# Maxima of cross-attention scores turned in two groups of 64 partitions, and modulation rows with the conditions stationary

## The chip, the core and the metric

The kernel runs on one core of a Trainium2 chip. A core has five engines, each with a queue of its own that is worked in order: TensorE (PE, with its weight loads PEld shown apart), VectorE (DVE), ScalarE (ACT), GpSimd (POOL) and SyncE (SP), which here issues DMAs. TensorE multiplies a stationary operand, loaded beforehand, by a moving one that streams past it, and writes to PSUM. A transpose ("turn" in the kernel) is such a product: the data stationary, a unit matrix moving.

The metric is device time in microseconds of the whole program.

## What is computed

One transformer block with adaptive layer norm: 16 batches of 224 tokens of width 512, 16 heads of 32, a context of 750 tokens. All in float32. Cut to what matters:

```python
c_proj = silu(c) @ W_mod + b_mod
shift_a, scale_a, gate_a, shift_m, scale_m, gate_m = split(c_proj, 6)
x_norm = ln(x) * (1 + scale_a[:, None]) + shift_a[:, None]
q, k, v = heads(x_norm @ W_qkv + b_qkv)
x = x + gate_a[:, None] * (heads_joined(softmax(q @ k.T * scale) @ v) @ W_proj + b_proj)
q_c = heads(ln(x) @ W_qc + b_qc)
k_c, v_c = heads(ln(context) @ W_kvc + b_kvc)
x = x + (heads_joined(softmax(q_c @ k_c.T * scale) @ v_c) @ W_cproj + b_cproj)
h = gelu((ln(x) * (1 + scale_m[:, None]) + shift_m[:, None]) @ W_mlp1 + b_mlp1)
x = x + gate_m[:, None] * (h @ W_mlp2 + b_mlp2)
```

The change touches two places: `c_proj`, and the maximum that the softmax of the cross attention takes over the 750 context tokens and subtracts before exp.

## The kernel before

It runs in four stages one after the other: a head (loads, modulation, first norms), self attention, cross attention, and the MLP. `Ordered` (line 22) keeps every engine's instructions in the order of the program; all of them are recorded on its line 28, so the profile is read by the names of the tiles. The `plan` dictionaries are a schedule written by hand: `at_slot` puts projections, norms and loads of the next step between the pieces of the present one.

**Modulation.** W_mod is loaded in six parts of 512 columns (`load_part`), two buffers for them. `make_part` (line 279) makes one part. Parts 2 and 5 are gates: the turned conditions `c_t` (128 x 16 per piece) are stationary and 512 columns of W_mod move; the rows get their bias and go to DRAM. Parts 0, 1, 3, 4 (shift and scale of attention and MLP) have W_mod stationary, in 16 blocks of 128 x 128, and the 16 columns of `c_t` moving, so that the result is at once by column (`mod_t`), 16 conditions wide. Parts 0 and 1 are made in the head (line 597), before x is turned and modulated (`turn_x`); 3 and 4 in slots of the first pair of batches. All biases come as rows into `brow` by five DMAs on ScalarE's queue at the start (line 138), and are turned to columns `bcol` by one transpose (line 270). `c_in`, the conditions, is loaded after them on the same queue; Silu of it, `c_act`, is then turned to `c_t`.

**Cross attention.** 64 units, 16 batches times 4 groups of 4 heads (`Unit`, line 964). A unit makes scores in three steps of two context chunks of 125 tokens: `scores(n)` with context tokens on the partitions, `keep(n)` folds them into the running maximum `top` (VectorE; 125 partitions, 4 heads x 224) and copies them to `pt` (ScalarE). At the unit's end `maxima` (line 1004) turns `top` by eight transposes of 125 partitions, in two PSUM banks one after the other, and reduces each bank on VectorE to `mc`, the negated maximum per head and token, with tokens on the partitions. `split_max` on GpSimd then writes it as three bfloat16 terms into three columns of `nmc`, whose other columns are zero.

In the next unit, the one before is worked on: `max_row` (line 1022) turns `nmc` by eight bfloat16 transposes, ScalarE copies the result to `mrow`, and `subtract(h)` (line 1031), once for each half of the heads, spreads it over 125 partitions by a bfloat16 product with ones (448 columns) and adds it to the three `pt` on VectorE. `weights(h)` takes exp on ScalarE and sums on GpSimd. One unit later still, `values` and `finish` make the output. So three units are in flight, and the order on every engine is the one of the loop at line 1085. PSUM: `sc` one buffer of four banks, `mm` three of one bank, `o` one.

Of the kernel before, what the change touches and what calls it, by code (L numbers as in the profile page):

```python
# [8 lines left out]
F32 = mybir.dt.float32  # L9
BF16 = mybir.dt.bfloat16  # L10
# [27 lines left out]
def kernel(  # L38
# [35 lines left out]
    CP = 125  # L74
    CC = S // CP
    CH = CC // 2
    PB = 2
    NP = B // PB
    PT = PB * TC
# [29 lines left out]
    nc.gpsimd.memset(ones16, 1.0)  # L109

    nms = []
    for i in range(3):
        t = const.tile([TP, TC, HG, HD], BF16, name=f"nm{i}")
        nc.gpsimd.memset(t, 0.0)
        nms.append(t)

    nmc = const.tile([TP, HG, TC, P], BF16, name="nmc")
    nc.gpsimd.memset(nmc, 0.0)  # L120

    def split_max(engine, nm, m):

        r = small.tile(list(m.shape), F32, name="rest")
        engine.tensor_copy(nm[:, :, :, 0], m)
        engine.tensor_tensor(r, m, nm[:, :, :, 0], ALU.subtract)
        engine.tensor_copy(nm[:, :, :, 1], r)
        engine.tensor_tensor(nm[:, :, :, 2], r, nm[:, :, :, 1], ALU.subtract)

# [3 lines left out]
    o_mlp = o_kvc + 2 * KC  # L135
    nbias = o_mlp + NF
    brow = const.tile([nbias, P], F32, name="brow")
    for off, vec in ((o_mod, b_mod), (o_qkv, b_qkv), (o_qc, b_qc), (o_kvc, b_kvc), (o_mlp, b_mlp1)):
        rows = vec.shape[0] // P
        nc.scalar.dma_start(out=brow[off : off + rows, :], in_=vec.rearrange("(r p) -> r p", p=P))  # L140
    bcol = const.tile([P, nbias], F32, name="bcol")

    def bias_rows(pool, vec, rows, name):
# [108 lines left out]
        xs[b] = load_x(sa, tokens(x, b), 6)  # L252
    load_part(1)
    wq, wk, wv = (load_w(ws, w_qkv[:, i * H : (i + 1) * H], f"wqkv{i}") for i in range(3))
    bg = mp.tile([B, 2, H], F32, name="bg", bufs=1)
    for i in range(2):
        lo = (2 + 3 * i) * H
        nc.scalar.dma_start(out=bg[:, i, :], in_=b_mod[lo : lo + H].partition_broadcast(B))

    c_act = mp.tile([B, H], F32, name="c_act", bufs=1)  # L260
    nc.scalar.activation(c_act, c_in, AF.Silu)

    c_t = mp.tile([P, KC, B], F32, name="c_t", bufs=1)
    ps = ps_mm.tile([P, 512], F32, name="mm")
# [1 line left out]
        turn(ps[:, k * B : (k + 1) * B], c_act[:, k * P : (k + 1) * P], ident[:B, :B])  # L266
    nc.vector.tensor_copy(c_t.rearrange("p k b -> p (k b)"), ps[:, : KC * B])

    ps = ps_mm.tile([P, 512], F32, name="mm")
    turn(ps[:, :nbias], brow, ident[:nbias, :nbias])  # L270
    nc.vector.tensor_copy(bcol, ps[:, :nbias])
    for i in (1, 4):
        sl = bcol[:, o_mod + i * KC : o_mod + (i + 1) * KC]
        nc.vector.tensor_scalar(sl, sl, 1.0, None, ALU.add)

    bqc = const.tile([P, KC], F32, name="bqc")
    nc.vector.tensor_scalar(bqc, bcol[:, o_qc : o_qc + KC], SCALE, None, ALU.mult)

    def make_part(i):
        w = w_part[i]  # L280
        ps = ps_mm.tile([P, 512], F32, name="mm")
        if i % 3 == 2:
            for k in range(KC):
                mm(ps[:B, :H], c_t[:, k, :], w[:, k, :], start=(k == 0), stop=(k == KC - 1))
            g = mp.tile([B, H], F32, name="gates", bufs=1)
            nc.vector.tensor_tensor(g, ps[:B, :H], bg[:, i // 3, :], ALU.add)
            nc.sync.dma_start(out=gate_d[i // 3], in_=g)
        else:
            slot = (i // 3) * 2 + i % 3
            for m in range(KC):  # L290
                for k in range(KC):
                    mm(
                        ps[:, m * B : (m + 1) * B], w[:, k, m * P : (m + 1) * P], c_t[:, k, :],
                        start=(k == 0), stop=(k == KC - 1),
                    )
            for m in range(KC):
                nc.vector.tensor_scalar(
                    mod_t[:, slot * KC + m, :], ps[:, m * B : (m + 1) * B],
                    bcol[:, o_mod + i * KC + m : o_mod + i * KC + m + 1], None, ALU.add,
                )  # L300
# [133 lines left out]
    if True:  # L434
# [70 lines left out]
        for p in range(NP):  # L505
            if p < NP - 1:
                for g in range(1, KC):
                    at_slot(p, 2 * g - 2, 0, lambda p=p, g=g: whole(project_qk(p, g)))
                    at_slot(p, 2 * g - 2, 1, lambda p=p, g=g: whole(project_qk(p, KC + g)))
                for t in range(PT if p else 0):  # L510
                    at_slot(p, 1 + t // 2 * 2, t % 2, lambda p=p, t=t: whole(project(p - 1, t)))
            else:

                left = [(project_qk, p, m) for m in (1, KC + 1, 2, KC + 2)]
                left += [(project, p - 1, t) for t in range(2)]
                left += [(project_qk, p, m) for m in (3, KC + 3)]
                left += [(project, p - 1, t) for t in range(2, PT)]
                parts = [h for f, *args in left for h in halves(lambda f=f, args=args: f(*args))]
                for i, h in enumerate(parts):
                    at_slot(p, i // 3, i % 3 // 2, h)  # L520
            if p == 0:
                at_slot(p, 1, 0, lambda: make_part(2))
                at_slot(p, 1, 1, lambda: make_part(3))
                at_slot(p, 1, 1, lambda: load_part(4))
                at_slot(p, 1, 1, lambda: load_part(5))
                at_slot(p, 3, 0, lambda: make_part(4))
                at_slot(p, 3, 1, lambda: make_part(5))
                at_slot(p, 3, 1, load_cross)
            n = p + 1
            if n < NP:  # L530
                if n > 1:
                    at_slot(p, 0, 0, lambda n=n: fetch(n))
                at_slot(p, 1, 0, lambda n=n: norm_begin(n))
                for t in range(PT):
                    at_slot(
                        p, 1 + t // 2, t % 2, lambda n=n, t=t: norms[PB * n + t // TC].stats(t % TC)
                    )
                for j in range(PB):
                    at_slot(p, 1 + j, 1, lambda n=n, j=j: norms[PB * n + j].apply())
                for k in range(KC):  # L540
                    at_slot(p, 4, k // 2, lambda n=n, k=k: turn_x(n, k))
                for t in range(PT):
                    at_slot(p, 5 + t // 2, t % 2, lambda n=n, t=t: project_v(n, t))
                at_slot(p, 7, 0, lambda n=n: whole(project_qk(n, 0)))
                at_slot(p, 7, 1, lambda n=n: whole(project_qk(n, KC)))

        def self_scores(p, g, j, nm):
# [12 lines left out]
                sc[:TP, :, : TC * N].rearrange("p s (c t) -> p s c t", c=TC),  # L560
                AX.X, ALU.max, negate=True,
            )
            split_max(nc.vector, nm, m)

        def self_weights(p, g, j, row):
            return weights_t(
# [27 lines left out]
        norm_begin(0)  # L594
        for j in range(PB):
            norms[j].all()
        make_part(0)
        make_part(1)
        load_part(2)
        load_part(3)  # L600
        fetch(1)
# [209 lines left out]
    with tc.tile_pool(name="ca", bufs=2, reuse_waits="tile") as ca:  # L811
# [152 lines left out]
        class Unit:  # L964
# [37 lines left out]
                self.pts.append(pt)  # L1002

            def maxima(self):
                m = small.tile([TP, HG, TC], F32, name="mc")
                for h in range(2):
                    ps = ps_mm.tile([P, 512], F32, name="mm")
                    for s in range(2):
                        for c in range(TC):
                            lo = (s * TC + c) * CP  # L1010
                            turn(
                                ps[:TP, lo : lo + CP], self.top[:, 2 * h + s, c * TP : (c + 1) * TP],
                                ident[:CP, :CP],
                            )
                    nc.vector.tensor_reduce(
                        m[:, 2 * h : 2 * h + 2, :],
                        ps[:TP, : 2 * TC * CP].rearrange("p (s c t) -> p s c t", s=2, c=TC),
                        AX.X, ALU.max, negate=True,
                    )
                split_max(nc.gpsimd, nmc, m)  # L1020

            def max_row(self):
                ps = ps_mm.tile([P, 1024], BF16, name="mm")
                for s in range(HG):
                    for c in range(TC):
                        lo = s * N + c * TP
                        turn(ps[:, lo : lo + TP], nmc[:, s, c, :], ident16[:TP, :TP])
                self.row = ca.tile([P, HG * N], BF16, name="mrow", bufs=1)
                nc.scalar.copy(self.row, ps[:, : HG * N])

            def subtract(self, h):

                bc = ps_o.tile([P, 512], F32, name="o")
                mm(
                    bc[:CP, : 2 * N], ones16[:, :CP], self.row[:, 2 * h * N : 2 * (h + 1) * N],
                    start=True, stop=True,
                )
                less = bc[:CP, : 2 * N].rearrange("p (s t) -> p s t", s=2).unsqueeze(2)
                for pt in self.pts:
                    w4 = pt[:, 2 * h : 2 * h + 2, :].rearrange("p s (k t) -> p s k t", k=2)  # L1040
                    nc.vector.tensor_tensor(w4, w4, less.to_broadcast([CP, 2, 2, N]), ALU.add)
# [43 lines left out]
        for b, g in units:  # L1085
# [2 lines left out]
                last.values()  # L1088
            for n in range(CH):
                st = cur.scores(n)  # L1090
                if n == 0 and prev:
                    prev.max_row()
                if n == 0 and last:
                    last.finish()
                cur.keep(n, st)
# [10 lines left out]
        sc = ps_s.tile([P, HG, 512], F32, name="sc")  # L1106
        prev.values()
        mlp_plain(sc[:, 0], 0)
        cur.max_row()
        prev.finish()  # L1110
        mlp_plain(sc[:, 1], 1)
        cur.subtract(0)
# [200 lines left out]
```

## Time and profile before

| | us |
|---|---|
| runs shown | 2943.93, 2943.95, 2952.13 (median 2943.95) |
| the profiled execution | 2940.97 |
| its span, first to last instruction | 2939.2 |
| mean granted clock of TensorE | 0.991 of full |
| turns of top: `mm<-ident,top`, 512 of 0.271 | 65.8 busy |
| turns of nmc: `mm<-ident,nmc`, 512 of 0.216 | 37.0 busy |
| products with ones: `o<-mrow,ones`, 128 of 0.355 | 45.4 busy |
| copies to mrow in cross attention (ScalarE), 64 of 0.906 | 58.0 busy |
| reductions to mc (VectorE), 128 of 0.669 | 85 busy |
| modulation, W_mod stationary: `mm<-c_t,w_mod`, 128 of 0.318 | 21.3 busy |
| modulation, conditions stationary: `mm<-w_mod,c_t`, 16 of 0.674 | 8.4 busy |

The profile gives groups of instructions as output<-inputs, with stationary rows*columns, and the moving shape. A float32 product is recorded as two instructions, a transpose as one. Durations of TensorE hold its pipeline's tail, so neighbours overlap; what a stream costs is read from start to start. A window's line gives the busy time of each engine in it, then the granted clock, the share of DMA time and GB/s. A wait's line says who waited for whom, how long in all, how often, and the longest.

### The profile page before, as it was taken

Reading aid. Unit: us, or ns where it says so; the run is one execution under the profiler, and the core shown is the slowest. Engines: PE = TensorE matmul, PEld = TensorE weight load, DVE = VectorE, ACT = ScalarE, POOL = GpSimd, SP = SyncE. Lnnn points to the kernel's source line nnn. Section 1 sums busy time; section 2 is a strip of 40 time slices with the busy share of each in tenths; the row PEclk is TensorE's granted clock in tenths of the full one; section 3 lists DMA queues with packets and bytes.
Section 4 is the critical chain, followed back from the end, with each engine's and each line's share of the span. In section 5 each row is a group of like instructions: output and inputs, shape, how many; then the busy total and the mean of one; then the engine's idle time right before and its main releaser. Section 6 shows DMA issues by size and latency. Waiting matters only on the chain.

```text
span 2939.2 us, 46558 instructions
## 1 busy us (share of the span) xinstructions
PE 2850.1 (97%) x19389; PEld 1829.9 (62%) x19389; DVE 1913.6 (65%) x2688; ACT 1175.4 (40%) x1462; POOL 1296.2 (44%) x1636
## 2 busy tenths in 40 slices
PE   8999999998999999999999999999978999999999
PEld 5544444444555565555656555555545888888888
DVE  3677766676478778777787777777775643443343
ACT  1222222221466665666566656665653022112211
POOL 1022222122367666676666766666564510221021
PEclk9999999999999999999999999999989999999999
DMA  5111110100100010100101100000012101111110
GB/s 189 59 32 32 32 32 11 59 11 26 54 32 24 22 35 24 34 28 19 34 24 34 35 18 28 26 33 24 22 44 99 55 30 49 43 47 30 54 44 29
DMA packets 55383, 114.40 MB, mean 39 GB/s; under 512 B 4308, under 2 KB 4372, under 8 KB 55172
## 3 DMA queue, kind: packets, MB, share of 16 engines
q1 hardware_dynamic: 54560, 110.58, 11.7%
q8 instruction: 152, 2.49, 0.4%
q10 hardware_dynamic: 612, 0.85, 0.1%
q14 instruction: 59, 0.48, 0.1%
HBM read 89.33 MB, written 22.09 MB: 38 GB/s over the span
## 4 chain that ended last, share of the span: by engine, by line
PE 80%; DVE 8%; issue 4%; ACT 4%; POOL 3%; DMA 1%; SPq 0%; ACTq 0%; POOLq 0%; DVEq 0%
PE mm L28 46%; PE a L28 10%; PE sc L28 9%; PE o L28 8%; PE b L28 5%; ACT pt L28 3%; PE c L28 3%; DVE at L28 2%; DVE top L28 2%; POOL acc L28 1%; DVE stats L28 1%; DVE m L28 1%; DVE mc L28 1%; ACT kt L28 1%; DMA gate<-gate_d 1%
## 5 line engine op out<-in xcount | busy, mean ns | idle before, releaser
L28 POOL TENSOR_TENSOR acc<-acc,pt 125x448 f32<-125x448 f32 x512 | 584.3, 1141 | 40.2
L28 DVE TENSOR_TENSOR pt<-pt,o 125x896 f32<-125x896 f32 x384 | 394.4, 1082 | 92.0 <-PE o L28 87.0
L28 ACT COPY pt<-sc 125x1792 f32<-125x1792 f32 x192 | 317.4, 1653 | 223.3 <-DVE top L28 199.0
L28 DVE TENSOR_TENSOR top<-top,sc 125x896 f32<-125x896 f32 x320 | 346.7, 1084 | 40.6 <-PE sc L28 34.0
L28 PE MATMUL mm<-wkvc,cxt 128*125 128x512 f32 x768 | 354.4, 604 | 8.6 <-ACT kt L28 8.6
L28 POOL TENSOR_TENSOR upd<-upd,gate 112x512 f32<-112x512 f32 (+1 forms) x60 | 78.9, 1315 | 632.5 <-DVE upd L28 627.8
L28 PE MATMUL mm<-cxt,wkvc 128*128 128x375 f32 x1024 | 350.5, 484 | 2.4 <-ACT cxt L28 2.4
L28 ACT ACTIVATE pt<-pt 125x896 f32<-125x896 f32 x384 | 339.1, 955 | 12.9 <-DVE pt L28 12.2
L28 POOL TENSOR_TENSOR acc<-pt 125x448 f32<-125x448 f32 x128 | 146.5, 1144 | 382.6 <-ACT pt L28 382.6
L28 DVE RECIPROCAL at<-o 128x224 f32<-128x224 f32 x128 | 198.8, 1553 | 102.1 <-PE o L28 102.1
L28 PEld LDWEIGHTS mm<-cxt,wkvc 128*128 128x128 f32 x1024 | 190.4, 191 | 112.7 <-issue 13.3
L28 PEld LDWEIGHTS mm<-wkvc,cxt 128*125 128x125 f32 x768 | 136.5, 187 | 175.2 <-issue 153.5
L28 ACT ACTIVATE pt<-sc 112x1792 f32<-112x1792 f32 x64 | 106.6, 1665 | 343.4 <-PE sc L28 338.8
L28 POOL TENSOR_TENSOR rstd<-mv,eps 112x2 f32<-112x2 f32 (+3 forms) x93 | 17.8, 192 | 475.5 <-DVE mv L28 475.5
L28 PE MATMUL sc<-qt,kt 32*125 32x224 f32 x3072 | 201.6, 377 | 12.9 <-ACT pt L28 12.3
L28 PE MATMUL mm<-xt,wqkv 128*128 128x448 f32 x512 | 209.0, 551 | 4.7 <-DVE xt L28 4.7
L28 DVE TENSOR_REDUCE m<-sc 112x8 f32<-112x1792 f32 x64 | 129.6, 2026 | 120.3 <-PE sc L28 120.3
L28 PEld LDWEIGHTS sc<-qt,kt 32*125 32x125 f32 x3072 | 132.9, 183 | 92.6 <-issue 41.0
L28 ACT COPY mrow<-mm 128x896 bf16<-128x896 bf16 x64 | 58.0, 906 | 309.2 <-PE mm L28 309.2
L28 PE MATMUL o<-pt,vt 125*32 125x224 f32 x3072 | 158.6, 355 | 0.0
L28 PEld LDWEIGHTS mm<-xt,wqkv 128*128 128x128 f32 x512 | 92.3, 190 | 86.7 <-issue 80.9
L28 ACT COPY mx<-a 128x512 f32<-128x512 f32 x26 | 15.3, 587 | 325.0 <-POOL upd L28 306.3
(192 smaller groups left out, 4846.7 us busy)
## 6 DMA issues: line engine op xcount, KB each, us to landing
cx<-in_ctx_dram SPq DMA_DIRECT2D x96, 250.0 KB
x<-in_x_dram SPq DMA_DIRECT2D x16, 448.0 KB
x_self<-x SPq DMA_DIRECT2D x16, 448.0 KB
x<-x_self SPq DMA_DIRECT2D x16, 448.0 KB
x_cross<-x SPq DMA_DIRECT2D x16, 448.0 KB
mx<-x_cross SPq DMA_DIRECT2D x28, 256.0 KB
w<-in_L_xcond_W_mlp_dram SPq DMA_DIRECT2D x7, 1024.0 KB
xr<-x_cross SPq DMA_DIRECT2D x28, 256.0 KB
```

The lines of the kernel that those rows point to most:

```text
L28: return lambda *args, **kw: self.tc.keep_in_program_order(f(*args, **kw))
```

## The change

Three edits go together.

- `maxima` turns `top` in two groups of partitions, 0 to 63 and 64 to 124, with turns of the two groups alternating and each group writing a bank of its own; each bank is reduced to a candidate (`mc0`, `mc1`), and the smaller of the negated candidates is `mc`.
- `max_row`, `nmc`, the GpSimd split and `mrow` of the cross attention go. `subtract` spreads the maximum by turning a column of `mc`, repeated 125 times by its access pattern, in float32: four turns a half.
- `make_part` becomes `part_rows` (conditions stationary for every part, the rows copied out of PSUM by ScalarE) and `finish_part` (four turns of the rows to columns, then the bias). Bias columns are made between the two in the head. `c_in` is the first load on ScalarE's queue and Silu follows it; the bias rows come after.

```diff
-    def make_part(i):
-        w = w_part[i]
+    def make_columns():
         ps = ps_mm.tile([P, 512], F32, name="mm")
+        turn(ps[:, :nbias], brow, ident[:nbias, :nbias])
+        nc.vector.tensor_copy(bcol, ps[:, :nbias])
...
+    def part_rows(i):
+
+        ps = ps_mm.tile([P, 512], F32, name="mm")
+        for k in range(KC):
+            mm(ps[:B, :H], c_t[:, k, :], w_part[i][:, k, :], start=(k == 0), stop=(k == KC - 1))
+        if i % 3 < 2:
+            r = mp.tile([B, H], F32, name="part", bufs=2)
+            nc.scalar.copy(r, ps[:B, :H])
+            return r
+        return ps
+
+    def finish_part(i, ps):
...
+            rows, ps = ps, ps_mm.tile([P, 512], F32, name="mm")
             for m in range(KC):
-                for k in range(KC):
-                    mm(
-                        ps[:, m * B : (m + 1) * B], w[:, k, m * P : (m + 1) * P], c_t[:, k, :],
-                        start=(k == 0), stop=(k == KC - 1),
-                    )
+                turn(ps[:, m * B : (m + 1) * B], rows[:, m * P : (m + 1) * P], ident[:B, :B])
...
+                at_slot(p, 1, 1, lambda: part(3))
...
+                at_slot(p, 2, 0, lambda: finish_part(3, made[3]))
+                at_slot(p, 3, 0, lambda: part(4))
+                at_slot(p, 3, 1, lambda: part(5))
+                at_slot(p, 3, 1, lambda: finish_part(4, made[4]))
...
-        make_part(0)
-        make_part(1)
+        rows = [part_rows(i) for i in range(2)]
+        make_columns()
+        for i in range(2):
+            finish_part(i, rows[i])
...
             def maxima(self):
...
+                parts = []
+                banks = [ps_mm.tile([P, 512], F32, name="mm") for _ in range(2)]
+                for s in range(HG):
+                    for c in range(TC):
+                        for i, (r, n) in enumerate(((0, RG), (RG, CP - RG))):
+                            lo = (s * TC + c) * n
                             turn(
-                                ps[:TP, lo : lo + CP], self.top[:, 2 * h + s, c * TP : (c + 1) * TP],
-                                ident[:CP, :CP],
+                                banks[i][:TP, lo : lo + n], self.top[r : r + n, s, c * TP : (c + 1) * TP],
+                                ident[r : r + n, r : r + n],
                             )
+                for i, n in enumerate((RG, CP - RG)):
+                    m = small.tile([TP, HG, TC], F32, name=f"mc{i}")
                     nc.vector.tensor_reduce(
-                        m[:, 2 * h : 2 * h + 2, :],
-                        ps[:TP, : 2 * TC * CP].rearrange("p (s c t) -> p s c t", s=2, c=TC),
+                        m, banks[i][:TP, : HG * TC * n].rearrange("p (s c t) -> p s c t", s=HG, c=TC),
                         AX.X, ALU.max, negate=True,
                     )
-                split_max(nc.gpsimd, nmc, m)
...
+                    parts.append(m)
+                self.m = small.tile([TP, HG, TC], F32, name="mc")
+                nc.vector.tensor_tensor(self.m, *parts, ALU.min)
+
+            def subtract(self, h):
+
+                bc = ps_o.tile([P, 512], F32, name="o")
+                for s in range(2):
                     for c in range(TC):
+
                         lo = s * N + c * TP
...
+                        col = self.m[:, 2 * h + s, c : c + 1].to_broadcast([TP, CP])
+                        turn(bc[:CP, lo : lo + TP], col, ident[:TP, :TP])
```

More of the change, by code (lines that the diff above doesn't have):

```diff
@@ L76 @@
     CH = CC // 2
+    RG = 64
     PB = 2
@@ L117, with split_max @@
         nms.append(t)
-    nmc = const.tile([TP, HG, TC, P], BF16, name="nmc")
-    nc.gpsimd.memset(nmc, 0.0)
-    def split_max(engine, nm, m):
+    def split_max(nm, m):
         r = small.tile(list(m.shape), F32, name="rest")
[L125 to L128, printed above, removed]
+        nc.vector.tensor_copy(nm[:, :, :, 0], m)
+        nc.vector.tensor_tensor(r, m, nm[:, :, :, 0], ALU.subtract)
+        nc.vector.tensor_copy(nm[:, :, :, 1], r)
+        nc.vector.tensor_tensor(nm[:, :, :, 2], r, nm[:, :, :, 1], ALU.subtract)
     o_mod, o_qkv = 0, 6 * KC
@@ L137 @@
     brow = const.tile([nbias, P], F32, name="brow")
-    for off, vec in ((o_mod, b_mod), (o_qkv, b_qkv), (o_qc, b_qc), (o_kvc, b_kvc), (o_mlp, b_mlp1)):
-        rows = vec.shape[0] // P
-        nc.scalar.dma_start(out=brow[off : off + rows, :], in_=vec.rearrange("(r p) -> r p", p=P))
     bcol = const.tile([P, nbias], F32, name="bcol")
@@ L254 @@
     wq, wk, wv = (load_w(ws, w_qkv[:, i * H : (i + 1) * H], f"wqkv{i}") for i in range(3))
+    c_act = mp.tile([B, H], F32, name="c_act", bufs=1)
+    nc.scalar.activation(c_act, c_in, AF.Silu)
+    for off, vec in ((o_mod, b_mod), (o_qkv, b_qkv), (o_qc, b_qc), (o_kvc, b_kvc), (o_mlp, b_mlp1)):
+        rows = vec.shape[0] // P
+        nc.scalar.dma_start(out=brow[off : off + rows, :], in_=vec.rearrange("(r p) -> r p", p=P))
     bg = mp.tile([B, 2, H], F32, name="bg", bufs=1)
@@ L258 @@
         nc.scalar.dma_start(out=bg[:, i, :], in_=b_mod[lo : lo + H].partition_broadcast(B))
-    c_act = mp.tile([B, H], F32, name="c_act", bufs=1)
-    nc.scalar.activation(c_act, c_in, AF.Silu)
     c_t = mp.tile([P, KC, B], F32, name="c_t", bufs=1)
@@ L267 @@
     nc.vector.tensor_copy(c_t.rearrange("p k b -> p (k b)"), ps[:, : KC * B])
[L269 to L274, printed above, removed]
     bqc = const.tile([P, KC], F32, name="bqc")
-    nc.vector.tensor_scalar(bqc, bcol[:, o_qc : o_qc + KC], SCALE, None, ALU.mult)
-    def make_part(i):
-        w = w_part[i]
+    def make_columns():
         ps = ps_mm.tile([P, 512], F32, name="mm")
+        turn(ps[:, :nbias], brow, ident[:nbias, :nbias])
+        nc.vector.tensor_copy(bcol, ps[:, :nbias])
+        for i in (1, 4):
+            sl = bcol[:, o_mod + i * KC : o_mod + (i + 1) * KC]
+            nc.vector.tensor_scalar(sl, sl, 1.0, None, ALU.add)
+        nc.vector.tensor_scalar(bqc, bcol[:, o_qc : o_qc + KC], SCALE, None, ALU.mult)
+    def part_rows(i):
[8 more added lines that the diff above has]
+    def finish_part(i, ps):
         if i % 3 == 2:
-            for k in range(KC):
-                mm(ps[:B, :H], c_t[:, k, :], w[:, k, :], start=(k == 0), stop=(k == KC - 1))
             g = mp.tile([B, H], F32, name="gates", bufs=1)
@@ L289, in make_part @@
             slot = (i // 3) * 2 + i % 3
+            rows, ps = ps, ps_mm.tile([P, 512], F32, name="mm")
             for m in range(KC):
-                for k in range(KC):
-                    mm(
-                        ps[:, m * B : (m + 1) * B], w[:, k, m * P : (m + 1) * P], c_t[:, k, :],
-                        start=(k == 0), stop=(k == KC - 1),
-                    )
+                turn(ps[:, m * B : (m + 1) * B], rows[:, m * P : (m + 1) * P], ident[:B, :B])
             for m in range(KC):
@@ L521, with part @@
             if p == 0:
-                at_slot(p, 1, 0, lambda: make_part(2))
-                at_slot(p, 1, 1, lambda: make_part(3))
+                made = {}
+                def part(i):
+                    made[i] = part_rows(i)
+                    if i % 3 == 2:
+                        finish_part(i, made[i])
+                at_slot(p, 1, 0, lambda: part(2))
+                at_slot(p, 1, 1, lambda: part(3))
                 at_slot(p, 1, 1, lambda: load_part(4))
                 at_slot(p, 1, 1, lambda: load_part(5))
-                at_slot(p, 3, 0, lambda: make_part(4))
-                at_slot(p, 3, 1, lambda: make_part(5))
+                at_slot(p, 2, 0, lambda: finish_part(3, made[3]))
+                at_slot(p, 3, 0, lambda: part(4))
+                at_slot(p, 3, 1, lambda: part(5))
+                at_slot(p, 3, 1, lambda: finish_part(4, made[4]))
                 at_slot(p, 3, 1, load_cross)
@@ L562, in self_scores @@
             )
-            split_max(nc.vector, nm, m)
+            split_max(nm, m)
         def self_weights(p, g, j, row):
@@ L1004, in maxima @@
             def maxima(self):
[L1005 to L1010, printed above, removed]
+                parts = []
[4 more added lines that the diff above has]
+                            lo = (s * TC + c) * n
@@ L1015, in maxima @@
                     nc.vector.tensor_reduce(
-                        m[:, 2 * h : 2 * h + 2, :],
-                        ps[:TP, : 2 * TC * CP].rearrange("p (s c t) -> p s c t", s=2, c=TC),
+                        m, banks[i][:TP, : HG * TC * n].rearrange("p (s c t) -> p s c t", s=HG, c=TC),
                         AX.X, ALU.max, negate=True,
                     )
-                split_max(nc.gpsimd, nmc, m)
-            def max_row(self):
-                ps = ps_mm.tile([P, 1024], BF16, name="mm")
-                for s in range(HG):
+                    parts.append(m)
@@ L1025, in max_row @@
+                self.m = small.tile([TP, HG, TC], F32, name="mc")
[3 more added lines that the diff above has]
+                for s in range(2):
                     for c in range(TC):
                         lo = s * N + c * TP
-                        turn(ps[:, lo : lo + TP], nmc[:, s, c, :], ident16[:TP, :TP])
-                self.row = ca.tile([P, HG * N], BF16, name="mrow", bufs=1)
@@ L1029, in max_row @@
[L1029 to L1037, printed above, removed]
+                        col = self.m[:, 2 * h + s, c : c + 1].to_broadcast([TP, CP])
+                        turn(bc[:CP, lo : lo + TP], col, ident[:TP, :TP])
                 less = bc[:CP, : 2 * N].rearrange("p (s t) -> p s t", s=2).unsqueeze(2)
@@ L1090 @@
                 st = cur.scores(n)
-                if n == 0 and prev:
-                    prev.max_row()
                 if n == 0 and last:
@@ L1108 @@
         mlp_plain(sc[:, 0], 0)
-        cur.max_row()
         prev.finish()
```

## The prediction

> **What bounds the kernel.** The page's first part, then busy time by stage.
>
> ```profile
> PE 2850.1 (97%) x19389; PEld 1829.9 (62%) x19389; DVE 1913.6 (65%) x2688; ACT 1175.4 (40%) x1462; POOL 1296.2 (44%) x1636
> 0.00:27.00 27.00, 17.57 (x86) 17.38 (x86) 9.18 (x27) 1.91 (x2) 8.54 (x26) 1.00 0.86 285
> 62.00:720.00 658.00, 641.73 (x5047) 321.28 (x5046) 462.55 (x759) 142.03 (x122) 133.88 (x164) 0.99 0.12 36
> 775.00:2215.00 1440.00, 1397.13 (x10600) 839.42 (x10602) 1104.35 (x1308) 876.41 (x1027) 972.96 (x1249) 0.99 0.09 28
> ```
>
> After the window come PE, PEld, DVE, ACT and POOL. TensorE is busy for 98% of self attention and 97% of cross attention, so a change there is worth what it takes from PE's stream or from PE's waits. The head (to 27 us) differs: PE works for 17.6 us only. The MLP behind 2245 us is not touched. The waits of PE in the cross window (total, times, longest):
>
> ```profile
> PE sc L28 <- ACT pt L28: 12.3, 5, 3.8
> PE mm L28 <- POOL nmc L28: 12.0, 16, 2.4
> PE mm L28 <- ACT kt L28: 8.6, 15, 0.6
> ```
>
> The timeline of one cross unit (of 64, some 22.5 us each) shows what is replaced:
>
> ```profile
> 1506.77 1.02 PE L28 MATMUL mm<-ident,top 125*112 125x125 f32 x8
> 1507.72 2.48 PE L28 MATMUL o<-pt,vt 125*32 125x224 f32 x48
> 1510.51 1.04 PE L28 MATMUL sc<-qt,kt 32*125 32x224 f32 x16
> 1511.47 0.41 PEld L28 LDWEIGHTS <-nmc 112*128 112x128 bf16 x8 [0.28 <-issue]
> 1511.88 2.75 PE L28 MATMUL mm<-cxt,wkvc 128*128 128x375 f32 x8
> 1514.47 0.35 PE L28 MATMUL o<-mrow,ones 128*125 128x448 bf16 x1
> 1514.66 2.69 PE L28 MATMUL mm<-cxt,wkvc 128*128 128x375 f32 x8
> ```
>
> [...]The turns of top hold PE from 1506.77 to 1507.72, 0.95 us; single starts in the trace lie 0.106 apart (125 columns), and 0.095 after the last one's columns the next form of tile begins. A bf16 product of 448 columns costs 1514.66 - 1514.47 = 0.19. The turns of nmc delay the projection by 0.41, less 0.05 of its own load that they hide: 0.36.
>
> **Cross attention, PE's stream, per unit.** Removed: the nmc turns, -0.36, and two bf16 products, -0.38. Added in subtract: two times four float32 turns, stationary 125 columns, moving 112. The nearest row:
>
> ```profile
> 102.38 0.93 PE L28 MATMUL mm<-ident,xn 112*128 112x112 f32 x8
> 103.24 0.96 PE L28 MATMUL o<-pt,v 112*32 112x224 f32 x16
> ```
>
> 0.86 less the 0.095 change of form is 0.765 for eight: 0.096 each, so 8 x 0.096 = +0.77, net +0.39. The load from one repeated column is in no row; below the row it can't go, since the 112 moving columns set it; above, I allow twice.
>
> Maxima: 16 turns of 64 (61) rows, moving 64 (61) columns, alternating between two groups of rows. By the row, 64 columns take 64/112 of 0.094 plus 0.002, 0.055. The scores show that groups of rows run together: four groups of 32 rows, 16 products of 224 columns in about 0.76 us, where one at a time they would take 16 x 0.19 = 3. Two groups then take 8 x 0.055 = 0.44. But a change of form now stands ahead of them, where the projection of q and the old turns shared one: 0.09, and 0.05 of a load that no product hides; behind them 0.095 as before. Sum 0.68 against 0.95: -0.27.
>
> Here two rules speak against the change. The Trainium skill, TensorEngine Tiling, Key Properties, says that changing the tiling mode drains the engine; the 0.09 above is that drain as this trace has it, and is charged. The page TensorE: Matmul & The Clock Gate, section LDWEIGHTS, prices a load at columns/1.2 ns: 93 for 112 columns, 104 for 125. By it the pairs would be bound by loads, 8 x 0.093, maxima 0.98 (+0.03) and subtract's turns 0.104 each (+0.45): +0.12 per unit, +8 us in all. But the xn turns load 128 columns and start every 96 ns, not 107, and in a lone case (single loads of cx at 1500.18 and 1500.24) the next load begins after 56 ns. I take the row: -0.36 + 0.39 - 0.27 = -0.24 per unit, **-15.4 us** over 64.
>
> **Waits.** The new chain is two reductions (0.67 each, as now), one small minimum (0.2, by the 112x8 rows of DVE) and the turn, which stands half a projection (2.6 us) later than the nmc turns did. GpSimd's four steps (0.9 us plus gaps) and ScalarE's copy of mrow (0.91) go. So the nmc waits, 12.0, and one of 1.0 on mrow end: **-13.0**. What is late next: (a) both PSUM banks are needed at once. In units 0 and 2 of each batch the second comes free when ScalarE has copied vt, 0.14 after the first turn begins; about 0.1 x 32 = 3.2. (b) In unit 1, VectorE's reductions end 4.2 us after the turns begin, and the minimum, then the reciprocal (1.56) and the top updates follow; the copy of pt after them ends about 0.3 later than PE, without its nmc wait, wants the bank: 4.8 over 16. (c) The kt waits grow by 0.1 x 15: 1.5. Given back: **+9.5**. ScalarE and GpSimd lose some 57 us each of work that was off the path; VectorE gains 13, hidden unless (b).
>
> **Head.** The chain of waits has ScalarE's five bias issues first, then
>
> ```profile
> 3.01 5.61 DMA c_in<-in_cond_dram
> 10.30 13.84 PE L28 MATMUL mm<-c_t,w_mod 128*128 128x16 f32 x64
> 80.61 3.75 PE L28 MATMUL mm<-c_t,w_mod 128*128 128x16 f32 x32
> 85.99 4.37 PE L28 MATMUL mm<-w_mod,c_t 128*16 128x512 f32 x7
> 81.60:85.00 3.40, 3.40 (x41) 3.35 (x44) 3.26 (x6) 0.00 (x0) 0.68 (x1) 1.00 0.00 0
> 85.00:88.40 3.40, 3.40 (x17) 0.68 (x10) 2.21 (x8) 1.66 (x1) 0.00 (x0) 0.50 0.00 0
> ```
>
> The same products with weights stationary take 0.216 each in the head, 0.117 later: half the clock, though the clock column says 1.00 (its first record is at 27 us). The last two lines (clock third from the end) show why: 3.4 us of these loads, with 16 columns moving, are followed by a granted clock of 0.50; 512-column products lift it again. The page named last, Part 1, says that about 3.4 us of busy PE release the clock; by that the head's two parts would cost 3.4 us at half speed and some 5.5 at full, 9 us, not 13.84. The row decides.
>
> New: c_in is issued first (lands near 3 instead of 8.6), c_t is there near 5; w_mod part 0 lands by 6.5 (ScalarE's issue that waits on it goes then), so part 0 starts at 6.5, not 10.3. Eight products of 512 columns a part: 0.86 each at half clock, 0.43 at full. Half clock until about 11.6: six products; two more to 12.5, when part 1 (landed at 12.6) follows at 0.43 x 8 = 3.4, to 16. Copy 0.6, four turns, mod_t 0.6 and the eight modulations (0.42 each) end near 21.3; the last quarter of the first projection ends at 22, now at 30. **-8**. Bounds -4 (ScalarE held behind the bias issues, each waiting for a landing, before it copies a part) and -10. Moved bias rows, gate biases, wproj and parts 2, 3 have over 5 us of cover: bcol is needed at 16, wproj at 38.
>
> **Self attention.** Parts 3 and 4 as 512-column products cost 8 x 0.43 = 3.44 for 3.7, plus four turns and two changes of form, net +0.3 each; the two stretches of half clock that their loads caused (3.4 us each, at 68 and 85) go: 2 x 1.7. **-2.8** (0 to -3.4). The ScalarE copies lie in an engine 22% busy.
>
> **Sum.** -15.4 - 13.0 + 9.5 - 8 - 2.8 = -29.7. The profiled execution took 2940.97 (span 2939.2): 2911.3. The median shown is 3.0 above it: **2914**.
>
> **Rivals.** (1) The waits take the saving back: VectorE's chain from the values to the copy of pt already sets 12.3 us of waits and has only 0.8 us of slack ahead of the second scores. Cross attention gains 2: 2944 - 13 = 2931. Against it: PE idles little, and no step of that chain grows but the minimum. (2) The groups do not overlap, but their loads hide: 16 x 0.055 + 0.24 = 1.12, +0.17, so the stream is +12.8 instead of -15.4, with no new waits: 2944 + 12.8 - 13 - 10.8 = 2933. (3) **Slower:** neither overlaps, each turn pays load and product, 0.049 + 0.055: 16 x 0.104 + 0.185 = 1.85, +0.90; stream +59.5; 2944 + 59.5 - 23.8 = 2980. It loses from 1.29 us for the maxima, 66 ns a turn. For it: no 64-row turn is in the trace. Against it: the scores. A slow load of the repeated column would need 0.23 us more per group of four (29.7 over 128 groups).
>
> **Chances.** Forecast 0.58; (1) 0.20; (2) 0.10; (3), with slow loads, 0.12. This kernel's runs can't tell 0.3% (8.8 us) from none. Faster: 0.58 + 0.15 + 0.05 = 0.78; within: 0.05 + 0.05 = 0.10; slower 0.12. Range 2898 to 2940: the forecast with a head of -10 and no waits given back at the lower end, (1) and (2) with a head of -4 at the upper; only (3) is outside.
>
> **What would show it.** Right: the turns of top span near 0.5 us by start times, the wait on nmc gone, the head's first projection at 18 to 19 us, granted clock 1.00 at 68 and 85. Wrong: maxima over 0.95 us from start to the values' start; subtract's turns over 0.11 each; PE's waits on ACT pt or vt above 25 us.

## The result and the profile after

The changed kernel took 2913.71 us (median of 2912.48 to 2915.22) beside 2946.26 for the kernel before on the same chip: a ratio of 0.989, 95% interval 0.9873 to 0.9907. The forecast was 2914, with a range of 2898 to 2940. Its profiled execution took 2912.48 us with a span of 2910.7.

The page's first part, three stages by window (fields as before), and the waits of PE in the cross window, all of the changed kernel:

```profile
PE 2833.8 (97%) x19693; PEld 1809.3 (62%) x19693; DVE 1929.8 (66%) x2752; ACT 1119.6 (38%) x1402; POOL 1241.7 (43%) x1379
0.00:20.50 20.50, 13.37 (x46) 4.59 (x46) 8.10 (x27) 3.06 (x4) 7.65 (x25) 1.00 0.93 300
55.50:712.00 656.50, 639.29 (x5007) 315.14 (x5006) 462.47 (x759) 143.02 (x124) 133.90 (x164) 0.99 0.12 36
767.00:2187.00 1420.00, 1387.67 (x10994) 837.75 (x10996) 1121.76 (x1371) 819.48 (x964) 920.07 (x997) 0.99 0.09 29
```

```profile
PE sc L28 <- ACT pt L28: 13.3, 17, 3.5
PE o L28 <- POOL acc L28: 7.0, 3, 3.7
PE mm L28 <- ACT kt L28: 6.9, 15, 0.5
```

PE is as busy as it was, in a shorter span; the wait on nmc is gone. Set beside the trace of before, from landmark to landmark:

| stretch | before | after | difference |
|---|---|---|---|
| to the first projection of q | 27.0 | 20.5 | -6.5 |
| from there to the first turn of top | 748.0 | 746.6 | -1.4 |
| first to last unit's turns of top | 1438.9 | 1418.8 | -20.1 |
| the rest of the span | 725.3 | 724.8 | -0.5 |

Unit 2 of a batch in the timeline of the changed kernel, the same kind of unit as the one shown of before:

```profile
1487.39 1.65 ACT L28 COPY pt<-sc 125x1792 f32<-125x1792 f32 x1 [0.83 <-POOL acc L28]
1487.76 1.68 PE L28 MATMUL mm<-xt,wqc 128*128 128x224 f32 x8
1488.94 0.59 ACT L28 COPY vt<-mm 125x512 f32<-125x512 f32 x1
1489.37 0.87 PE L28 MATMUL mm<-ident,top 64*112 64x64 f32 x16
1490.16 2.48 PE L28 MATMUL o<-pt,vt 125*32 125x224 f32 x48
1492.95 1.04 PE L28 MATMUL sc<-qt,kt 32*125 32x224 f32 x16
1493.91 2.79 PE L28 MATMUL mm<-cxt,wkvc 128*128 128x375 f32 x8
1496.54 0.59 PE L28 MATMUL o<-ident,mc 112*125 112x112 f32 x4
1496.97 2.71 PE L28 MATMUL mm<-cxt,wkvc 128*128 128x375 f32 x8
```

From scores to projection it is 0.96 us (1493.91 - 1492.95) where it was 1.37: no turns of nmc between. The column turns cost 0.43 (1496.97 - 1496.54) where the product with ones cost 0.19. From turns to values it is 0.79, was 0.95. It would be less, but ScalarE's copy of vt, which holds the second bank, ends only at 1489.53. In units without that wait the single starts in the trace give 0.58 to 0.59.

### The profile page after: what moved, and what is told of

Same layout as the page of the kernel before. It is cut to its first block, busy times and chain, and to the rows that moved or that the text cites. A ratio compares the mean times of both kernels' runs of the same rounds, so it can differ in the third digit from the quotient of the medians.

```text
span 2910.7 us, 46976 instructions
## 1 busy us (share of the span) xinstructions
PE 2833.8 (97%) x19693; PEld 1809.3 (62%) x19693; DVE 1929.8 (66%) x2752; ACT 1119.6 (38%) x1402; POOL 1241.7 (43%) x1379
## 4 chain that ended last, share of the span: by engine, by line
PE 79%; DVE 10%; ACT 5%; issue 4%; POOL 2%; DMA 1%; SPq 0%; POOLq 0%; ACTq 0%; DVEq 0%
PE mm L28 43%; PE a L28 10%; PE sc L28 10%; PE o L28 8%; PE b L28 5%; ACT pt L28 4%; DVE at L28 3%; PE c L28 3%; DVE top L28 2%; POOL acc L28 1%; DVE stats L28 1%; DVE m L28 1%; DVE mc L28 1%; ACT kt L28 1%; DMA gate<-gate_d 1%
## 5 line engine op out<-in xcount | busy, mean ns | idle before, releaser
L28 PEld LDWEIGHTS mm<-cxt,wkvc 128*128 128x128 f32 x1024 | 184.7, 190 | 118.9 <-issue 15.4
L28 DVE TENSOR_REDUCE mc<-mm 112x8 f32<-112x512 f32 (+1 forms) x128 | 79.8, 666 | 98.4 <-PE mm L28 98.3
```

Source lines behind the costliest of these rows:

```text
L28: return lambda *args, **kw: self.tc.keep_in_program_order(f(*args, **kw))
```

## Experiments

All times are medians, each beside runs of the kernel before on the same chip. There were three sets of runs: groups undone, order of the turns, q first and the copied column in the first, the modulation and the queue's order in the second, the copy by VectorE, the width and both of these in the third. The kernel before had 2946.7, 2942.5 and 2944.8 in them. The changed kernel ran again in the second and third; runs of the first are compared with its 2913.71 of the result. A unit's period is the time from its first turn of top to that of the next unit, as the median over the batches.

**The changed kernel again.**

> The changed kernel as it is, beside the two parts: 2914 by every theory.

> The changed kernel as it is, on the same chip beside these: 2914.

2913.9 us (ratio 0.990, 0.9887 to 0.9914) and 2914.85 (0.9902, 0.9887 to 0.9917). Its three medians lie within 1.2 us and its single runs within 4.4, so no difference of medians under 3 us is read below.

**One part alone: the modulation.** The kernel before with the new `part_rows`, `make_columns`, `finish_part` and the new order of the first loads; its maxima, `nmc` and `mrow` stay.

> The kernel before with only the modulation part of the change (rows with conditions stationary, order of the first loads). Theory: head -6.5 and self attention -1.4 as the trace of the changed kernel has them, 8 us faster than before: 2938. Rival (the cross stage, not these, holds most of what was gained, and an earlier head is waited for later): 0 to 2 us faster.

2933.46 us, ratio 0.9969 (0.9957 to 0.998): 9.0 us faster, where 8 were expected. The first projection starts at 20.1 us in its trace, and the cross stage is as before (1439.2 us from first to last turns). So the head's gain isn't waited for later, and the cross edits hold the other 20 (2933.46 - 2913.9).

**Only the order on ScalarE's queue.**

```diff
-    for off, vec in ((o_mod, b_mod), ...):
-        nc.scalar.dma_start(out=brow[off : off + rows, :], ...)
...
+    nc.scalar.activation(c_act, c_in, AF.Silu)
+    for off, vec in ((o_mod, b_mod), ...):
+        nc.scalar.dma_start(out=brow[off : off + rows, :], ...)
     bg = mp.tile([B, 2, H], F32, name="bg", bufs=1)
...
```

> The kernel before with only the order on ScalarE's queue changed: conditions and Silu first, bias rows after. Theory: PE starts part 0 at 7.0 instead of 10.3 us, its 64 small products still go at half clock, 0.216 each, and the first projection of q starts near 24 instead of 27: 3 us faster than before. Rival (the clock is up once PE starts earlier, or the later bias rows hold the head up): the clock full before 20 us and 8 us faster, or no gain.

2943.87 us, ratio 1.0009 (1.0 to 1.0018): no gain. PE's timeline in this run:

```profile
4.74 0.58 PE L28 MATMUL mm<-ident,c_act 16*128 16x16 f32 x4 [4.74 <-ACT c_act L28]
11.84 0.36 PE L28 MATMUL mm<-ident,brow 64*128 64x64 f32 x1 [6.52 <-DMA brow<-in_L_xcond_b_mlp_dram]
12.13 13.83 PE L28 MATMUL mm<-c_t,w_mod 128*128 128x16 f32 x64
28.83 3.70 PE L28 MATMUL mm<-xt,wqkv 128*128 128x448 f32 x9
```

The conditions are turned 4.7 us earlier, but PE's queue has the turn of the bias rows next, and their last DMA now lands so late that PE idles 6.5 us; the projection starts at 28.8, later than before. The forecast of 3 us had missed this; the rival had named it. The 64 records of small products take 13.83 us as ever, so their pace isn't a matter of when they start. In the change, `make_columns` stands behind the parts, and part 0 starts at 6.97.

**The groups undone.** The changed kernel with eight turns of 125 partitions.

```diff
-                banks = [ps_mm.tile([P, 512], F32, name="mm") for _ in range(2)]
...
+                for h in range(2):
+                    ps = ps_mm.tile([P, 512], F32, name="mm")
...
+                                ps[:TP, lo : lo + CP], self.top[:, 2 * h + s, c * TP : (c + 1) * TP],
+                                ident[:CP, :CP],
```

> The changed kernel with the maxima turned as before (eight turns of 125 partitions, two banks one after the other, no minimum); column turns and modulation stay. Theory (PE's stream sets the time): from PE's last projection to the values the maxima go back from 1.08, 1.24, 1.08, 0.87 us (units 0 to 3 of a batch) to 1.14, 1.64, 1.14, 1.14, which is 0.78 per batch: about 12 us slower than the changed kernel, 2925. Rival (VectorE's chain paces the units, the shorter turns only end in a wait): 0 to 3 us slower, 2914 to 2917.

2923.83 us (ratio 0.9926, 0.9914 to 0.9939), some 10 us slower than the changed kernel where 12 were expected: the theory, nearly whole. What is missing sits in unit 1. Its path from projection to values is 0.39 us longer than with groups (1.63 against 1.24), its period only 0.05 (22.73 against 22.68): with groups PE then waits 0.17 for ScalarE's copy of pt ahead of the second scores, 13 times, and here never. In units 0, 2 and 3 the periods are longer by 0.15, 0.06 and 0.26.

This run also parts the two cross edits. From the first to the last unit's turns of top it takes 1428.2 us, the modulation alone 1439.2 and the changed kernel 1418.8. So about 11 us come from the way by nmc and mrow that went, and 9 from the groups.

**The order of the turns.** All of one group first, then all of the other.

```diff
-                for s in range(HG):
-                    for c in range(TC):
-                        for i, (r, n) in enumerate(((0, RG), (RG, CP - RG))):
+                for i, (r, n) in enumerate(((0, RG), (RG, CP - RG))):
+                    for s in range(HG):
+                        for c in range(TC):
```

> The same 16 turns, but all eight of partitions 0 to 63 first, then all eight of 64 to 124. Theory (the saving is the overlap of neighbours in different groups of rows): the turns go one after the other at 0.055 us, 0.88 instead of 0.44 from first to last; the wait for the second bank (0.21 in units 0 and 2) is then covered. So +0.44 in units 1 and 3, +0.23 in units 0 and 2, some 64 x 0.33 = 21 us slower than the changed kernel: 2935. Rival (short moving operand alone saves, the order doesn't matter): 2914, or 2908 with the wait covered.

2921.94 us (ratio 0.9917, 0.9903 to 0.993): 8 us slower than the changed kernel, not 21. The direction is the theory's; the rival falls. Single starts show why it is less: the first turn of the second group starts 0.28 us after the first of all, between the fifth and the sixth of the first group. PE takes it ahead of three older turns; that it does so because its rows are free is my guess. So the groups overlap for a while in this order too, and first to last is 0.71 us, not 0.88. From projection to values it is 1.14 in three units of four, what the eight full turns cost. So in those units the short moving operand saves nothing without the alternation.

**The stall on the second bank, by the order of PE.** In units 0 and 2, q is projected ahead of v.

```diff
-                    at_slot(b, g, (5, 3, 5, 5)[g], lambda f=f, m=m: project_q(f, m))
+                    at_slot(b, g, (4, 3, 4, 5)[g], lambda f=f, m=m: project_q(f, m))
```

(and the projections of v in those units a slot later)

> The changed kernel with the projection of q moved ahead of the projection of v in the last two slots of units 0 and 2, so that the second bank of the maxima is the one of q, free 3 us earlier. Theory: the stall of 0.21 us after the first turn in 31 units goes, 6.5 us faster than the changed kernel: 2907. Rival: the time is only waited for elsewhere (ScalarE's copy of pt ahead of the second scores): 2914.

2913.56 us (2909.68 to 2918.01): inconclusive. In the trace the stall falls from first to last turn (0.65 to 0.51, not to 0.44), and the periods of units 0 and 2 by 0.14 and 0.13, two thirds of the 0.21 expected; some 4 us in all, which the runs don't resolve.

**The same stall, by another engine.** PE's order stays; VectorE copies v out of PSUM in the slot ahead of those maxima.

```diff
+            if by_vector:
+                nc.vector.tensor_copy(vt[b, c], ps[:CP, :H])
+            else:
                 nc.scalar.copy(vt[b, c], ps[:CP, :H])
```

> The changed kernel with the projection of v in the slot ahead of the maxima of units 0 and 2 copied out of PSUM by VectorE, which is idle there, instead of ScalarE, whose copy waits behind the copy of pt. PE's order stays. Theory: the second bank is free in time, first to last turn in units 0 and 2 falls from 0.65 to 0.44, periods of units 0 and 2 from 21.52 and 22.82 to some 21.3 and 22.6, 6 us faster than the changed kernel: 2908. Rival (VectorE's chain sets the pace): no change or slower, with longer waits of PE on ScalarE's copy of pt.

2909.23 us (ratio 0.9883, 0.9867 to 0.9899), 5.6 us faster than the changed kernel beside it. Unit 2 in its timeline:

```profile
1485.86 1.65 ACT L28 COPY pt<-sc 125x1792 f32<-125x1792 f32 x1 [0.83 <-POOL acc L28]
1486.42 0.69 DVE L28 COPY vt<-mm 125x512 f32<-125x512 f32 x1 [0.67 <-PE mm L28]
1487.82 0.66 PE L28 MATMUL mm<-ident,top 64*112 64x64 f32 x16
1488.41 2.48 PE L28 MATMUL o<-pt,vt 125*32 125x224 f32 x48
```

VectorE copies while ScalarE is still at pt, the bank is free 0.7 us early, and from turns to values it is 0.59 instead of 0.79. Periods of units 0 and 2 are 21.31 and 22.61 (21.52 and 22.83 beside it): the stall was on the path, with its full 0.21. The rival, a longer wait elsewhere, falls.

**Why a column turn costs 0.107 us and not 0.096: the repeated column?**

```diff
+                self.cols = ca.tile([TP, HG * TC, CP], F32, name="cols", bufs=1)
+                nc.gpsimd.tensor_copy(self.cols, ...to_broadcast([TP, HG * TC, CP]))
...
-                        col = self.m[:, 2 * h + s, c : c + 1].to_broadcast([TP, CP])
+                        col = self.cols[:, (2 * h + s) * TC + c, :]
```

> GpSimd writes the repeated column out (112 x 8 x 125) and subtract's turns load from that tile instead of from one column by a repeating pattern. Theory (the repeating pattern loads slower): starts of those turns 0.096 us apart instead of 0.107, weight loads 0.14 long instead of 0.188; 128 groups of four gain 0.04 each, 5 us: 2909. Rival (any float32 load of 125 columns goes at 0.107): starts stay at 0.107, time 2914. If GpSimd, busier by 1.2 us a unit, comes onto the path: slower than 2914, with waits on GpSimd in PE's list.

2914.36 us, starts still 0.107 apart, weight loads 0.189 long. The repeating pattern costs nothing here; the theory falls.

**Or its width of 125?**

```diff
-                        col = self.m[:, 2 * h + s, c : c + 1].to_broadcast([TP, CP])
-                        turn(bc[:CP, lo : lo + TP], col, ident[:TP, :TP])
+                        col = self.m[:, 2 * h + s, c : c + 1].to_broadcast([TP, P])
+                        turn(bc[:, lo : lo + TP], col, ident[:TP, :TP])
```

> The changed kernel with subtract's turns loading the repeated column 128 times instead of 125 (three rows of the output more, which nobody reads). Theory now (the width sets it: the full width of 128, as the xn turns have it, loads in half the time of 125): starts 0.096 apart instead of 0.107, weight loads 0.14 instead of 0.188, 128 groups gain 0.04 each where PE sets the pace, up to 5 us: 2909 to 2912. Rival (a column narrower in memory than what is read, or this operand itself, sets it, whatever the width): starts 0.109, as 128 columns at the same rate cost, 2914 to 2915.

The instructions of the tile mc, changed kernel, then this run (durations shortest/median/longest in ns):

```profile
L28 PEld LDWEIGHTS o<-ident,mc x512: 182/188/334, 771.3 to 2200.4; 112*125 112x125 f32 x171
L28 PE MATMUL o<-ident,mc x512: 259/272/417, 771.6 to 2200.5; 112*125 112x112 f32 x171
```

```profile
L28 PEld LDWEIGHTS o<-ident,mc x512: 132/135/230, 773.1 to 2200.7; 112*128 112x128 f32 x171
L28 PE MATMUL o<-ident,mc x512: 257/258/394, 773.4 to 2200.8; 112*128 112x112 f32 x171
```

Three columns more load 0.05 us faster, and starts are 0.095 apart, as in the xn turns. The time, 2915.07 (ratio 0.99, 0.9885 to 0.9915), shows no gain: with PE ahead, the waits on ScalarE's kt rise from 6.9 to 8.4 us in the cross stage, and the periods of units 0 to 3 shrink by 0.08, 0.03, 0 and 0.08, not by 0.08 each.

**Both last edits.**

> Both edits of e8 and e9. Theory: their gains add, 2903 to 2906 if both hold. Rival: the second gain ends in the wait of the scores for ScalarE's copy of pt, no better than the better one of the two.

2905.44 us (ratio to before 0.9868, 0.9853 to 0.9883; runs from 2902.47 to 2907.65), under every run of the changed kernel beside it (2914.81 to 2916.32) and 9.4 us faster: the best version here. The second edit is worth 3.8 on top of the first, in medians; the periods are 21.23, 22.64, 22.61 and 22.37.

## Why the prediction was right, point by point

The mechanism held: the overlap of the two groups, the end of the wait on nmc and the clock in the head and in self attention all show in the traces. That 2914 was met by 2913.71 is closer than the sizes were, and in that part luck. In cross attention the stream gave some 2 us less than priced and the waits as much more, which cancels; head and self attention gave 2.9 less. From one profiled execution to the other the gain is 28.5 us where 29.7 were forecast; between medians it is 32.5 here and 28.6 and 30.0 in the later sets, since the kernel before varies. The range is wider than its stated terms: they give 2902.5 (2914 - 2 - 9.5) and 2937 (2933 + 4). And 0.3% could be told from none: the modulation alone is 0.31%, with an interval that leaves out 1.

- **Maxima, -0.27 per unit.** In unit 3, which has no stall, the way from projection to values went from 1.138 to 0.870 us: -0.268. The first turn starts 0.095 later behind the projection than before, the change of form as priced. The 16 turns span 0.44 by starts: in each group the second starts 0.105 after the first, the others 0.056 apart, so the 0.05 for the first load shows there. The undone groups (+10 us) and the order by group show that it is the overlap. So the drain that the Trainium skill (TensorEngine Tiling, Key Properties) tells of was right to charge, though no run here parts it from other causes of the 0.095. The load price of columns/1.2 ns (its TensorE: Matmul & The Clock Gate, LDWEIGHTS), which would have taken the whole gain away, does not hold at 112 columns: by it loads take 0.093, and turns with such loads start 0.056 us apart in each group.
- **The turns of nmc, -0.36 per unit.** Too small. In the units without a wait it is 1.372 us from the scores' start to the projection before and 0.967 now: -0.405. The 0.05 of the projection's own load that I set against it is not lost; 3 us over 64 units.
- **Column turns, +0.39 per unit.** Too small: 0.425 for four, 0.85 per unit, +0.47, 5 us more over 64 units. The row of the xn turns did not carry over to 125 columns; there 0.104 by that load price was the better one (0.107 measured). At 128 columns the row holds again. With the two terms before it the stream is -0.405 + 0.47 - 0.27, or -0.2 per unit, -13 in all.
- **Waits that go, -13.0.** Gone, both. Unit 1 shows it alone: from the scores behind its turns to the projection it took 2.07 us, 0.70 more than in the other units, and its period fell by 0.75. In the last batch other waits of PE shift (at 1.2 us more, acc 0.4 more, pt 1.2 less) and nearly cancel.
- **Waits that come, +9.5.** In size, too much: 0.21 x 31 = 6.5 on the second bank (I had 0.1 each, 3.2, and put the free time of the bank without the drain); 2.2 in the 13 waits on ScalarE's pt (I had 4.8); those on kt shrank by 1.7 (I had +1.5). Together 7.0.
- **Cross stage.** Predicted -15.4 - 13.0 + 9.5 = -18.9. The terms as measured give -13 - 13.0 + 7.0 = -19.0. The trace of the changed kernel has -20.1, its traces in the second and third set -18.2 and -20.0. They differ in the first and the last batch alone. The longest unit of the last took 29.15 us before (granted clock 0.82 in it), and 26.17 (0.87), 28.62 (0.82) and 26.21 in the three traces now. Batch by batch in between, the periods of units 0 to 3 fell by 0.02, 0.75, 0.03 and 0.27: in units 0 and 2 the stall on the second bank takes the saving back.
- **Head, -8.** Measured -6.5, and the sign set for it, a first projection at 18 to 19 us, was missed: it starts at 20.50.

```profile
6.97 9.81 PE L28 MATMUL mm<-w_mod,c_t 128*16 128x512 f32 x16 [1.54 <-DMA w_mod<-in_L_xcond_W_mod_dram]
18.64 3.43 DVE L28 TENSOR_SCALAR xt<-mm,mod_t 128x224 f32<-128x224 f32 x8
20.50 6.25 PE L28 MATMUL mm<-xt,wqkv 128*128 128x448 f32 x16 [0.22 <-PE mm L28]
```

  Part 0 starts at 6.97 (predicted 6.5), the full clock is there at 12.1 by its first record (11.6), and the two parts end at 16.6 by starts (16), part 1 having waited for its weights until 13.17. The eight modulations begin 2.0 us behind that, about as priced (21.3 - 8 x 0.42 is 1.9 behind 16), and end at 22.1 (21.3). The step that was mis-sized is the last: I had the first projection end 0.7 behind the modulations, at 22, and it ends at 23.6, 1.5 behind. Its eight records take 3.1 us, and they start only at 20.50, just after the fourth modulation ends at 20.39. That fits a PSUM bank that comes free then; no run tests it.
- **Self attention, -2.8.** Measured -1.4. The half clock is gone: from 12.1 to 701 us the granted clock stays at 1.00, and so do both windows that had 0.50,

```profile
85.00:88.40 3.40, 3.40 (x15) 1.92 (x14) 3.26 (x6) 0.00 (x0) 0.00 (x0) 1.00 0.57 195
68.00:71.40 3.40, 3.12 (x8) 1.44 (x8) 3.33 (x10) 1.00 (x1) 0.00 (x0) 1.00 0.00 0
```

  (of the changed kernel, whose work lies some 6.5 us earlier). But PE waits 0.8 for qk in the second window, 0.4 at most before, while VectorE is busy for 3.33 of 3.4 us; the other 0.6 is not traced. Head and self attention together: -10.8 predicted, -7.9 in the trace, -9.0 in the runs of the modulation alone.
- **Rivals.** Waits that take the saving back: in small, in units 0, 1 and 2. The 12.3 us of waits on pt that this rival was drawn from were misread: they lie in the last batch alone, and between 750 and 2130 us the kernel before has none. No overlap, and slow loads of the repeated column: excluded by the trace and by the copied column.

## What to carry to other kernels

Small products that use half of the rows gained here only where neighbours in the program lay in different groups of rows; each group also had a bank of its own, and one bank for both was not tried. Check, for each bank, which engine frees it last, and give that copy to an engine that is idle there. Moving one load ahead in a queue moves others back: the early conditions gained nothing while the work that waits for the displaced loads stood ahead of the parts. And a price from a near row holds for that row's shape: 125 columns and 128 were not the same load.

## What the runs showed that was not expected

- A float32 load for a turn takes 0.135 us (median) at 128 columns and 0.188 at 125; by starts 0.095 against 0.107. Loads of 112 columns are short too (0.131). Reading one column 125 times costs the same as reading a copy (0.188 and 0.189). No other widths were tried.
- PE starts a turn of the other group of rows ahead of three older ones of the first, so order by group still gives overlap: 0.71 us for 16 turns, 0.44 with alternation.
- 64 records of 16 moving columns take 13.83 us in the head whether they start at 10.30 or 12.13, while of 16 records of 512 columns in their place the first six start some 0.85 us apart and the second part's 0.43: the clock is full within some 5 us of their start at 6.97.
